# Written program order for the load queue and GpSimd, projection weights asked for one by one, and no emptying of the list of score portions at a period's end

## The chip, the cores and the metric

One Trainium2 chip; the kernel runs on one core of it. The metric is the device time of one execution in microseconds (us), as the median over several executions. In what follows PE is TensorE, DVE is VectorE, ACT is ScalarE, POOL is GpSimd, and SP is SyncE, which here only issues DMAs: it is the queue of nearly all loads.

## What is computed

Two cross-attention layers over 8 batches (B) of 100 queries (S) with 640 channels (C), 20 heads of 32, all in float32. The context has 722 tokens of 1024 channels, of which the first 77 are text and the other 645 image tokens ("ip"), with their own key and value weights. Layer 0 is

```python
q = heads(x @ Wq.T)
out_text = attend(q, heads(text @ Wk.T), heads(text @ Wv.T), 1 / sqrt(D))
out_ip   = attend(q, heads(ip @ Wk_ip.T), heads(ip @ Wv_ip.T), 1 / sqrt(D))
out = (out_text + out_ip) @ Wo.T + bo + x
```

with `attend` a softmax over the keys and the product with the values. Layer 1 does the same with its own weights on layer 0's output, with two differences: to the scores of the image tokens it adds a term that is the same for all heads (a softmax of the text attention over all channels, carried over to the image tokens by their products with the text), and a mask of the 100 queries multiplies the image part.

## The kernel before

**Units and periods.** A unit is a layer with a batch: 16 of them (`u`), each with five chunks of four heads (`c`), so 80 periods (`ORDER`, L44). The main loop (L1571 to L1661) goes through the periods. In each, it does the attention of one chunk, and between its pieces it places a share of the products that make the later units' keys and values.

**Products.** Keys and values of the image tokens are made by a scheme of seven products in place of eight, used twice: an outer one (`OUTER`) over quarters of the operands, and within it `seven` (L152). `v_steps` (L465, matmuls at L479) and `k_steps` (L516, matmuls at L525) are its inner products, `fifth_steps` (L541, L554) do what is left over. Sums of input tokens are DVE's (L258 to L264, L281 to L287), the results leave PSUM through ACT (L176) and DVE (L179), and the outer sums are POOL's (L441). POOL's queue also writes the finished keys and values to DRAM (`put`, from L381) and the sums of weights (`ol_d`, `tx_d` and the like) in the first stage.

**Loads.** Weights stream through six buffers of the tag "w"; `take` (L314) asks for weights up to five ahead of the one that PE is about to use, all on SP (L329, L348, L361, L375). In layer 0 some of them get a second DMA into the same tile, the text columns (L340). SP also loads token tiles (`load_a`, L235 and L238), q of a unit (`load_q`, L1106), text values (L1112, L1113), keys and values of a period (`load_k`, L1120 and L1121, with two buffers; `load_v`, L1126), and projection weights (`load_wo`, L1212), which `out_piece` (L1215) and `q_piece` (L1235) use through three buffers of the tag "wo". Where SP reaches a DMA whose buffer or source isn't ready, it waits, and every load behind it waits too.

**Who sets the order.** The program is written under `manual_schedule(engines=PINNED)` (L1039 for the first stage, L1571 for the body). For the engines in `PINNED` (L47) the instructions run in the order in which the program asks for them; for the others a scheduler chooses. Before, PE, DVE and ACT are pinned, and SP and POOL are not.

**A period.** `scores` (L1300) part 0 makes the scores of the first 512 keys of four heads, part 1 those of the other 210 (133 image and 77 text). Each part uses the same two tiles of PSUM banks, `sc0` and `sc1`, for two heads each, so the next part's matmuls (L1312) wait until all that reads the former part's banks is done. Right behind the matmuls only `maxima(0)` is asked for (layer 0: a reduction, L1321; layer 1: a fused add, minimum and accumulate into `p`, L1327). The rest is put into the list `later` as portions with a flag. The flag is true where the portion reads the `sc` banks:

- part 0: `maxima(1)` (true), exponentials of heads 0 and 1 (true), of heads 2 and 3 (true; ACT, L1335)
- part 1: `maxima(1)` (true), text maxima with differences and exponentials (true; L1342, L1344, L1351, L1352), exponentials of heads 2 and 3 with those of the text (true in layer 0 alone; L1335, L1357, L1360), the last text exponentials (true in layer 0 alone), `factors` (false; L1367 to L1371), and `widened` with `scaled_rest` (false; POOL L1377, ACT L1388, DVE L1383)

`next_task` (L1579) asks for one portion whenever products of 1.0 us or more, by the planner's own costs, have gone by since the last one. `free_scores` (L1296) asks for all up to the last one that is flagged true. The transposes of the former period's probabilities go to PSUM in six steps (`transposes`, L1432; copied out by ACT at L1440 for steps 0, 2, 4 and 5, by DVE at L1442 for steps 1 and 3), and `values` (L1444, matmuls L1454) multiplies them with the values; its results go through DVE (L1459, L1460). A period is, in this order: scores part 0; products up to 0.4; transposes 0 and 1 of the former period; products up to 0.6; transposes 2 and 3; scores part 1; products up to 0.8; the loads of this period's values and the next one's keys; transposes 4 and 5; products up to 1.0; values of the former period. In the last periods there are no products.

Before, the list is emptied three times in a period: ahead of transposes 0 (`emit(len(later))` at L1424), ahead of the values (L1650) and behind them (L1653); `free_scores` is called ahead of the second scores only.

## Time and profile before

| | |
|---|---|
| median of 3 runs | 2092.13 us (2086.02 to 2099.58) |
| profiled execution | 2102.3 us; span 2100.5 us; mean granted clock of TensorE 0.979 |
| PE busy | 1971.8 us (94%) |
| first stage of sums and text products, and units ahead of the body | 0 to about 552 us |
| body, layer 0 | about 552 to 1449 us (40 periods) |
| body, layer 1 | 1449 us to the end (40 periods) |
| DMA | 419.13 MB, mean 200 GB/s |

The page first gives each engine's busy time, then the span in 40 slices of 52.5 us, in which a digit is the busy share in tenths; PEclk is the clock that TensorE was granted, in tenths of full speed. A line of a group reads: line, engine, operation, output and inputs, shape, count, then busy time, mean ns of one, and idle time of the engine just ahead of them with what ended it. A line of waits reads: who waited, for what, then total us, times, and the longest. The two busy PE figures by stage, from a table of windows: 277.80 us of the 331 from 219 to 550 us (clock 0.94), 871.06 of the 899 from 550 to 1449 us (clock 0.99), 607.05 of the 651 from there to 2100 us (clock 0.98).

### The profile page before, as it was taken

How to read it: one execution, taken by the hardware profiler on the slowest of the kernel's cores; microseconds unless marked ns; L12 is line 12 of the kernel's file. 1: busy time of each engine (PE TensorE's matmuls, PEld its weight loads, DVE VectorE, ACT ScalarE, POOL GpSimd, SP SyncE). 2: the span in 40 equal slices, each digit the busy share in tenths (PEclk: the TensorE clock that was granted, in tenths of full speed). 3: DMA queues.
4: the chain of work that ended last, by engine and by line, in shares of the span. 5: the costliest groups of instructions: out<-in, count | busy, mean ns of one | idle time of the engine just before them, and what ended most of it. 6: DMA issues, size and time to landing. Idle time of an engine off the chain costs nothing. (4 is left out here: it accounts for less than half of the span.)

```text
span 2100.5 us, 43283 instructions
## 1 busy us (share of the span) xinstructions
PE 1971.8 (94%) x15422; PEld 1608.4 (77%) x15422; DVE 1231.7 (59%) x3047; ACT 829.0 (39%) x2839; POOL 1039.9 (50%) x1256
## 2 busy tenths in 40 slices
PE   9999876899999999999999999999999999999998
PEld 8676765787777788778788888887877777676787
DVE  2322673554655754665457666657676666766666
ACT  1001000010244443544354435445554555556665
POOL 2788887545456452644445674663455355210110
PEclk9999998999999999999999999999999999999999
DMA  9577887777666667766776676666766666554441
GB/s 350 204 264 262 263 278 231 199 215 213 201 183 197 201 178 205 212 189 181 204 226 197 205 216 205 202 204 177 211 187 200 178 200 194 149 159 119 137 132 53
DMA packets 439600, 419.13 MB, mean 200 GB/s; under 512 B 67691, under 2 KB 381819, under 8 KB 439131
## 3 DMA queue, kind: packets, MB, share of 16 engines
q1 hardware_dynamic: 407982, 306.67, 50.7%
q0 software_dynamic: 26400, 101.03, 13.4%
q10 hardware_dynamic: 5004, 8.68, 1.1%
q8 instruction: 124, 2.03, 0.4%
q14 instruction: 90, 0.73, 0.1%
HBM read 315.07 MB, written 101.18 MB: 198 GB/s over the span
## 5 line engine op out<-in xcount | busy, mean ns | idle before, releaser
L441 POOL TENSOR_TENSOR cv<-cv,cv 128x320 f32<-128x320 f32 x252 | 219.7, 897 | 305.0 <-DVE cv L179 280.3
L1440 ACT COPY pt<-pspt 128x400 f32<-128x400 f32 x320 | 156.1, 491 | 226.2 <-PE pspt L1432 225.5
L441 POOL TENSOR_TENSOR ck<-ck,ck 128x256 f32<-128x256 f32 (+1 forms) x252 | 201.0, 803 | 67.9 <-DVE ck L179 44.4
L1432 PE MATMUL pspt<-ident,p 100*128 100x100 f32 (+1 forms) x1920 | 210.1, 252 | 19.3 <-ACT pt L1440 7.1
L1432 PEld LDWEIGHTS pspt<-ident,p 100*128 100x128 f32 (+1 forms) x1920 | 189.4, 139 | 50.5 <-issue 14.9
L1335 ACT ACTIVATE p<-sc,st 100x512 f32<-100x512 f32 (+1 forms) x320 | 166.6, 533 | 71.5 <-DVE st L1342 49.2
L1335 ACT ACTIVATE p<-p,st 100x512 f32<-100x512 f32 (+1 forms) x320 | 177.1, 557 | 11.7 <-DVE st L1327 9.3
L1377 POOL COPY wide<-st 100x128 f32<-100x128 f32 x80 | 30.4, 380 | 292.8 <-DVE st L1371 265.2
L479 PE MATMUL psv_d<-w,i 128*128 128x160 f32 (+1 forms) x1008 | 170.0, 312 | 3.2 <-DMA w<-text_t 1.0
L479 PEld LDWEIGHTS psv_d<-w,i 128*128 128x128 f32 x1008 | 154.3, 193 | 14.8 <-issue 3.0
L176 ACT COPY cv<-psv_a 128x320 f32<-128x320 f32 x126 | 53.7, 426 | 262.6 <-PE psv_a L479 241.7
L1312 PE MATMUL sc<-k,q 32*100 32x210 f32 (+1 forms) x1280 | 149.2, 507 | 8.2 <-ACT p L1360 7.0
L176 ACT COPY ck<-psk_a 128x256 f32<-128x256 f32 (+1 forms) x126 | 47.2, 374 | 256.9 <-PE psk_a L525 209.1
L1388 ACT ACTIVATE p<-p,st 100x133 f32<-100x133 f32 x316 | 102.3, 395 | 115.5 <-DVE st L1371 115.4
L525 PE MATMUL psk_d<-i,w 128*128 128x256 f32 (+1 forms) x504 | 134.6, 390 | 10.6 <-DMA w<-op_dk 6.0
L1327 DVE CUSTOM_DVE_ANT_0 p<-sc,sem 100x512 f32<-100x512 f32 (+1 forms) x320 | 139.5, 489 | 1.3 <-PE sc L1312 1.3
L1442 DVE COPY pt<-pspt 128x400 f32<-128x400 f32 x160 | 91.6, 573 | 73.6 <-PE pspt L1432 72.7
L1321 DVE TENSOR_REDUCE st<-sc 100x2 f32<-100x1024 f32 (+1 forms) x160 | 126.6, 824 | 7.7 <-PE sc L1312 7.3
L525 PEld LDWEIGHTS psk_d<-i,w 128*128 128x128 f32 x504 | 92.5, 192 | 37.4 <-issue 16.2
L479 PE MATMUL psv_a<-w,a 128*128 128x160 f32 (+1 forms) x576 | 107.1, 330 | 5.2 <-DVE ck L179 5.0
L179 DVE TENSOR_TENSOR cv<-psv_d,cv 128x320 f32<-128x320 f32 x126 | 61.6, 489 | 82.0 <-PE psv_d L479 80.7
L479 PEld LDWEIGHTS psv_a<-w,a 128*128 128x128 f32 x576 | 93.7, 196 | 12.3 <-DVE ck L179 5.3
(278 smaller groups left out, 4409.6 us busy)
## 6 DMA issues: line engine op xcount, KB each, us to landing
w<-op_dv SPq DMA_DIRECT2D x252, 160.0 KB
a<-ip_t SPq DMA_DIRECT2D x33, 1024.0 KB
w<-op_dk SPq DMA_DIRECT2D x252, 128.0 KB
k<-k_d SPq DMA_DIRECT2D x80, 322.5 KB
v<-v_d SPq DMA_DIRECT2D x80, 320.0 KB
v_d<-cv POOLq DMA_DIRECT2D x28, 640.0 KB, 4.9
w<-os_dv SPq DMA_DIRECT2D x108, 160.0 KB
k_d<-ck POOLq DMA_DIRECT2D x28, 512.0 KB, 4.5
```

The lines of the kernel that those rows point to most:

```text
L176: nc.scalar.copy(c11, flat(bank))
L441: nc.gpsimd.tensor_tensor(to[:, a, b], of[:, a, b], other[:, a, b], ALU.add)
L479: nc.tensor.matmul(ps[:, o * pitch : o * pitch + m], lhsT=of[:, kc, o * w : o * w + P], rhs=wt[:, kc, :], start=(o == 0 and kc == 0 and no ...
L525: nc.tensor.matmul(ps[:, : 2 * w], lhsT=wt[:, kc, :], rhs=of[:, kc, :], start=(kc == 0 and not go_on), stop=(kc == 1), skip_group_check=True,)
L1312: nc.tensor.matmul(scs[i // 2][:S, i % 2, : k1 - k0], lhsT=qs_[u][rows, c, :], rhs=ks[u, c][rows, k0:k1], start=True, stop=True)
L1321: nc.vector.tensor_reduce(st[:, part, 2 * h : 2 * h + 2], scs[h][:S, :, :n], AX.X, ALU.max, negate=True)
L1327: nc.vector.tensor_tensor_reduce(out=p[:, i, k0 : k0 + n], in0=scs[h][:S, i % 2, :n], in1=sems[u][:, k0 : k0 + n], scale=-1.0, scalar=3.0e ...
L1335: nc.scalar.activation(dst, dst if l else scs[h][:S, i % 2, :n], AF.Exp, bias=st[:, part, i : i + 1], scale=-1.0 if l else 1.0, accum_out= ...
L1388: nc.scalar.activation(p[:, i, KA:NI], p[:, i, KA:NI], AF.Copy, scale=mul[:, 1, i : i + 1])
L1432: nc.tensor.transpose(ps[:rows, i * S : (i + 1) * S], pr[u, c][:, i, j * P : j * P + rows], ident[:S, :S])
L1440: nc.scalar.copy(dst, src)
L1442: nc.vector.tensor_copy(dst, src)
```

## The change

Three parts.

1. `PINNED` holds SP and POOL as well: their DMAs and POOL's sums run in the written order.
2. `load_wo` puts its weights on a list `wo_next`, and `fill_wo` issues a load only while one of three places is free; a place becomes free when `out_piece` or `q_piece` has been asked for. Before, all of a group's loads were asked for at once, and the scheduler placed them. The loads of one group come at the start of periods 0 and 1 of an even unit (`loads`, L1543).
3. `scores` calls `free_scores` ahead of both parts. The list is no longer emptied ahead of transposes 0, nor around the values, except in the last period.

```diff
-PINNED = {mybir.EngineType.PE, mybir.EngineType.DVE, mybir.EngineType.Activation}
+PINNED = {
+    mybir.EngineType.PE, mybir.EngineType.DVE, mybir.EngineType.Activation, mybir.EngineType.SP, mybir.EngineType.Pool
+}
...
+    wo_next, wo_free = [], [3]
+
     def load_wo(kind, src, g, chunks=range(NC_)):
-        for c in chunks:
+        wo_next.extend((kind, src, g, c) for c in chunks)
+        fill_wo()
+
+    def fill_wo(done=0):
+        wo_free[0] += done
+        while wo_next and wo_free[0]:
+            kind, src, g, c = wo_next.pop(0)
+            wo_free[0] -= 1
             t = one.tile([P, NC_, P], F32, tag="wo", name=f"{kind}_{g}_{c}", bufs=3)
...
             nc.gpsimd.dma_start(x1_d[g], res)
+        fill_wo(1)
...
             nc.gpsimd.dma_start(q_d[1][g], qst[g])
+        fill_wo(1)
...
             stats[u, c] = stat.tile([S, 11, 4], F32, tag="st", name=f"st_{u}_{c}")
-        else:
-            free_scores()
-
+        free_scores()
...
     def transposes(u, c, j, at_end=False):
         if j == 0:
-            emit(len(later))
             pts[u, c] = one.tile([P, 6, 4 * S], F32, tag="pt", name=f"pt_{u}_{c}")
...
-            emit(len(later) - (n == len(ORDER) - 1))
+            if n == len(ORDER) - 1:
+                emit(len(later) - 1)
             if last:
                 values(*last)
-            emit(len(later))
+            if n == len(ORDER) - 1:
+                emit(len(later))
             last = (u, c)
```

## The prediction

> **What bounds the kernel now.** I read the page's busy shares first, then its slices, then the groups of instructions, the waits of TensorE (PE), the timeline of one period and the waits of the load queue (SP).

> ```profile
> span 2100.5 us, 43283 instructions
> PE 1971.8 (94%) x15422; PEld 1608.4 (77%) x15422; DVE 1231.7 (59%) x3047; ACT 829.0 (39%) x2839; POOL 1039.9 (50%) x1256
> PE   9999876899999999999999999999999999999998
> PEclk9999998999999999999999999999999999999999
> ```
> PE is the bound: 94% busy at full clock nearly everywhere, no other engine over 59%. Only slices 5 to 8 (about 210 to 420 us) show room. So a wait that the change puts on PE is paid in full, and little can be won.

> ```profile
> PE psv_e L479 <- DMA w<-op_dv: 22.5, 6, 15.2
> PE sc L1312 <- ACT p L1360: 7.0, 5, 2.1
> PE sc L1312 <- DVE st L1327: 1.2, 2, 0.6
> ```
> Adding up PE's gaps: 124 us in 101, of which 53 us in 219–550 us (45 us on loads) and some 68 us behind it, 41 us on DVE and 15 us on ACT. The scores (L1312) wait for nearly nothing in 160 instances: their banks are free in time.

> ```profile
> L1327 DVE CUSTOM_DVE_ANT_0 p<-sc,sem 100x512 f32<-100x512 f32 x160 | 101.4, 684 | 0.6 <-PE sc L1312 0.6
> L1442 DVE COPY pt<-pspt 128x400 f32<-128x400 f32 x160 | 91.6, 573 | 73.6 <-PE pspt L1432 72.7
> ```
> These are what can come between PE and its next scores: the maxima of layer 1 and the copy of a transposed tile.

> ```profile
> 1508.51 0.91 PE L1432 MATMUL pspt<-ident,p 100*128 100x100 f32 x8
> 1509.35 0.61 PE L1312 MATMUL sc<-k,q 32*100 32x210 f32 x8
> 1509.45 0.57 DVE L1442 COPY pt<-pspt 128x400 f32<-128x400 f32 x1 [0.72 <-PE pspt L1432]
> 1509.99 0.30 DVE L1327 CUSTOM_DVE_ANT_0 p<-sc,sem 100x133 f32<-100x133 f32 x1
> ```
> Today the second scores follow the transposes without a gap: all four maxima of the first part were done long before.

> **The change, part by part.** PE's order is the same instruction by instruction; on DVE, ACT, POOL and SP the counts stay and the order moves.

> *Portions: scores, part 1, layer 1.* The emptying at L1424 came ahead of transposes 0. Without it a portion is asked for only per 1.0 us of product, and layer 1's periods are shorter (40 in 651 us, against 40 in 897 us). Following the list through the loop, task by task with the planner's own times (0.87 to 1.35 us a product, so at most one portion for two), the second maxima of part 0 are still unasked at `scores(…, 1)` in 33 of 40 periods. `free_scores` asks for them there, so on DVE they stand behind the copy of transposes 3, which ends 0.60 us after those transposes. Two maxima at 0.61 us pace and the last read make 1.30; the first two heads' scores (0.28) run meanwhile: 0.60 + 1.30 − 0.28 = 1.6 us for PE. Where leftovers of the period before are ahead of them, DVE does those first: L1383 adds 0.47, the whole of L1367 to L1383 1.6 us (1800.80 to 1802.40). By lists: 9 × 1.65, 3 × 2.1, 18 × 3.2, 3 × 4.2, and 1.7 in the rest = **+93 us**. Below: 33 × 1.0 if DVE runs ahead (33); above: 40 × 4.2 (168). I take 93, from this row's own pace.

> *Scores, part 0, layer 1.* In 11 periods text maxima are left over, and stand on DVE behind the two hs operations (L1459, L1460), which wait for the values: 7 × 1.7 + 4 × 1.2 = 17, less 2 of cover: **+15** (0 to 30).

> *Layer 0.* At part 1, exponentials are left in 11 periods. ACT does four at 0.73 us behind the copy of transposes 2: 6 × 1.3 + 3 × 2.7 + 2 × 3.1 = 22, and 2 at part 0: **+24** (0 to 40; the waits on L1360 today, 1.4 us each, are the low side).

> *Last eight periods.* No products lie between, so transposes 4 and 5 wait for what ACT is asked for late (four L1388 at 0.32 pace, exponentials): **+10** (0 to 20).

> *Clock.* Of about 25 gaps of 1.6 us or more in this trace, 16 are followed by a stretch at half clock, for instance after the 2.48 us that ended at 1426.58:
> ```profile
> 1426.00:1428.00 2.00, 1.42 (x8) 1.11 (x8) 2.00 (x6) 1.77 (x5) 1.40 (x1) 0.92 0.01 4
> 1428.00:1430.00 2.00, 1.95 (x8) 1.89 (x8) 2.00 (x3) 0.48 (x2) 2.00 (x3) 0.50 0.33 80
> 1430.00:1432.00 2.00, 2.00 (x13) 1.99 (x12) 1.36 (x4) 0.24 (x1) 1.39 (x2) 0.73 0.06 18
> ```
> The last but two column is the clock. Such a stretch of some 3.4 us loses 1.7. The parts above make about 38 such gaps; 38 × 16/25 × 1.7 = **+41 us** (0 to 65).

> [...]

> *What goes.* The burst at a period's end put maxima, exponentials, factors and scaling on DVE and ACT at once, ahead of values. The gaps behind 550 us that DVE and ACT end are 56 us, with some ten clock drops. I take half of the gaps and a few drops: **−35** (0 to −60).

> *SP and GpSimd in written order; what stands behind each wait.*
> ```profile
> SPq L340 <- DMA w<-op_dv: 32.9, 29, 3.2
> SPq L1106 <- DMA ol_d<-olv: 15.5, 1, 15.5
> SPq L1120 <- PE sc L1312: 95.3, 67, 8.5
> SPq L1126 <- PE pv L1454: 78.7, 65, 15.0
> SPq L1212 <- PE pspt L1432: 39.9, 24, 4.8
> ```
> Each of these holds every later load. (a) q's load (L1106) blocks SP for 15.5 us and gave PE its longest gap, 15.16 at 342.08. In the written order it stands further back, but still ahead of a unit's weights, and its source is still written by POOL behind four adds of 0.87 and eight of 0.69: some 12 us of block in place of 15. (b) The block of 299–317 us (4.25 + 3.24 + 3.64 = 11 us) comes from two activations' loads held by DVE; they now stand together: about 4 us. (c) The text columns (L340) stand right behind their weight's load, into the same tile; each holds SP for 2.7 us (750.63 to 753.31). Four in a row outrun a look-ahead of five weights when products are 2.4 us: +10 in the first stage, 0 to 5 in the body, where I take 0. (a) to (c) with other first-stage loads that move: **−8** (−28 to +15). (d) k (L1120) is asked for at 0.8 of the period before, and comes 4.3 to 6 us before its scores, where v and k (643 KB) need 4 us if they flow at the 161 GB/s that layer 1 moves in the mean, and 5.5 if a quarter of that is weights (an estimate): **+3** (0 to 25). (e) A projection weight (L1212) now waits for its piece at most some 3 us, which five weights of look-ahead cover: **0** (0 to 3); cover gone, its cost is those 3 us per piece.

> **Sum.** 93 + 15 + 24 + 10 + 41 − 35 − 8 + 3 = +143 us. The profiled execution took 2102.3 (span 2100.5, 1.8 around it), 0.5% above the runs' median of 2092.1. 2102.3 + 143 = 2245; against the median **2235**.

> **The rivals.**
> *1. Faster: the end of the period gives more than the scores take.* If the new stalls in layer 1 are 1 us with their clock in place of (93 + 41)/33 = 4.1, because DVE reaches the copy before PE has need of it, they cost 33; 15 of the smaller stalls stay; the burst's gaps and drops go whole (56 + 10 × 1.7 = 73), and 8 on SP: 33 + 15 − 73 − 8 = −33, **2060**. It decides below about 2 us per stall. For it: DVE is only 59% busy, and 41 us of gaps end on DVE. Against: the copy cannot start before PE has done transposes 3, and PE's next instruction are the scores.
> *2. The clock holds.* As the main case without the 41: **2194**. For it: a third of today's gaps cost no clock; against: the row above.
> *3. SP becomes the bound.* k late by 25 us in all, text columns +5, the first stage at +15: 143 − 3 + 25 + 5 + 23 = +193, **2285**. For it: one queue, with 67 waits of L1120; against: SP's waits today end before PE's need nearly always.
> *4. Nothing much.* If portions were still asked for in time the rest is −8 + 3 and the time stays at **2090**. The order on DVE speaks against it.

> **How the numbers follow.** Main case 0.53, rival 2 0.20, rival 3 0.10, rival 1 0.10, rival 4 0.07. The likeliest gives 2235. The range leaves out rivals 1 and 4 and the outer part of 3: from 2115 (the low ends of the scores and the clock: 33 + 0 + 10 + 0 + 0 − 20 = +23) to 2290. About 1% is what a measurement of this kernel can tell from no change: faster 0.10, same 0.07, slower 0.83.

> **What would show it.** Right: PE's sc L1312 waiting on DVE L1327 some 35 times for about 90 us; some 20 us of sc on ACT L1335; a clock below 0.95 in slices from about 1450 us; one long L1106 wait in the first stage; waits of PE on DVE and ACT in products (ck, cv L179) down. Wrong: sc's waits under 1 us each; no half clock behind them; or PE's gaps in layer 1 ended by DMA (k, w), which would be rival 3.

## The result and the profile after

| | before | changed |
|---|---|---|
| median of 4 runs each | 2095.86 us (2086.02 to 2100.02) | 2377.03 us (2372.31 to 2381.6) |
| ratio | | 1.1349, 95% interval 1.1296 to 1.1402 |
| profiled execution: span, mean granted clock | 2100.5 us, 0.979 | 2371.4 us, 0.932 |

The changed kernel is 13.5% slower, 281 us by the medians. The forecast was 2235 us, with a range up to 2290: the direction was right, the rise that it gave was half of the measured one, and 2377 us lies above the range. Lines of the changed kernel have other numbers: L479 is L481, L340 is L342, L1106 is L1108, L1312 is L1323, L1327 is L1338, L1432 is L1442, L1442 is L1452.

The page of the changed kernel, top and slices:

```profile
span 2371.4 us, 43269 instructions
PE 2092.5 (88%) x15422; PEld 1692.2 (71%) x15422; DVE 1231.6 (52%) x3047; ACT 825.7 (35%) x2839; POOL 1025.7 (43%) x1256
PE   9999989786889998998899989999898998888877
PEclk9999999988999998999999999999999999888877
```

PE does the same 15422 instructions in 2092.5 us of busy time where it took 1971.8. DVE, ACT and POOL are as busy as before to within 1.5%. So PE has lost time in two ways: it waits more, and the same work takes longer. The clock row says why the work takes longer: in the last six slices it stands at 8 or 7, where it was 9 before.

The waits of PE in the changed kernel (who waited, for what; us in total, times, longest):

```profile
PE sc L1323 <- DVE st L1338: 87.8, 34, 3.8
PE sc L1323 <- DMA k<-k_d: 28.6, 14, 5.7
PE psv_e L481 <- DMA w<-tx_d: 22.0, 7, 7.5
PE psv_a L481 <- DMA w<-text_t: 21.4, 2, 20.3
PE sc L1323 <- ACT p L1346: 19.7, 17, 1.8
PE sc L1323 <- issue: 12.2, 7, 1.8
```

The scores, which waited for nearly nothing before, now have four main causes of waiting. To see the whole, I added up PE's idle time stage by stage, and the clock that was not granted ("clock lost": one minus the clock, added up over time, so that a microsecond at half clock counts 0.5):

| stage | before | changed | longer by | more idle | more clock lost |
|---|---|---|---|---|---|
| ahead of the first scores | 551 us | 575 us | 23 | 15 | 12 |
| layer 0 | 894 | 986 | 92 | 60 | 31 |
| layer 1, 32 periods | 547 | 640 | 93 | 44 | 43 |
| last 8 periods | 108 | 170 | 62 | 32 | 32 |
| sum | 2100.5 | 2371.4 | 271 | 150 (129 to 279) | 117 (45 to 162) |

The two columns account for 267 of the 271 us (stage by stage to within 6). One second score of layer 1 shows both losses. First the timeline, from the transposes to the scores (start, duration, engine, line; brackets: idle ahead of it):

```profile
1611.22 0.85 PE L1442 MATMUL pspt<-ident,p 100*128 100x100 f32 x8
1612.01 0.60 PE L1323 MATMUL sc<-k,q 32*100 32x210 f32 x4
1612.11 0.57 DVE L1452 COPY pt<-pspt 128x400 f32<-128x400 f32 x1 [1.96 <-PE pspt L1442]
1612.61 0.47 DVE L1378 TENSOR_REDUCE st<-p 100x4 f32<-100x308 f32 x1
...
1613.76 0.47 DVE L1394 TENSOR_TENSOR p<-p,st 100x308 f32<-100x308 f32 x1
1614.15 0.68 DVE L1338 CUSTOM_DVE_ANT_0 p<-sc,sem 100x512 f32<-100x512 f32 x1
...
1615.50 1.02 PE L1323 MATMUL sc<-k,q 32*100 32x210 f32 x4 [2.90 <-DVE st L1338]
```

The first two heads' scores go ahead. DVE, which had idled for 1.96 us, then does the copy, the factors, and only then the two maxima that free the other bank: 2.90 us for PE. Next the same place in stretches of 3.41 us (length, PE's busy time first, the granted clock third from the end):

```profile
1610.86:1614.27 3.41, 1.75 (x16) 1.25 (x14) 2.05 (x8) 1.17 (x4) 0.30 (x1) 1.00 0.98 339
1614.27:1617.68 3.41, 2.18 (x8) 1.64 (x9) 2.13 (x12) 3.41 (x11) 0.11 (x1) 0.50 0.11 41
1617.68:1621.10 3.42, 3.42 (x11) 3.06 (x11) 0.40 (x1) 0.79 (x3) 0.35 (x1) 0.50 0.27 72
1621.10:1624.51 3.41, 3.41 (x28) 3.38 (x28) 0.03 (x1) 1.84 (x7) 3.41 (x5) 1.00 0.71 229
```

The one gap lies in two of these stretches, 1.66 us in the first and 1.23 in the second, and each is followed by one at half clock. The gap cost 2.90 us of idle and 3.4 of clock.

### The profile page after: what moved, and what is told of

Same layout as the page of the kernel before. It is cut to its first block, busy times and chain, and to the rows that moved or that the text cites. A ratio compares the mean times of both kernels' runs of the same rounds, so it can differ in the third digit from the quotient of the medians.

```text
span 2371.4 us, 43269 instructions
## 1 busy us (share of the span) xinstructions
PE 2092.5 (88%) x15422; PEld 1692.2 (71%) x15422; DVE 1231.6 (52%) x3047; ACT 825.7 (35%) x2839; POOL 1025.7 (43%) x1256
## 5 line engine op out<-in xcount | busy, mean ns | idle before, releaser
L1323 PE MATMUL sc<-k,q 32*100 32x210 f32 (+1 forms) x1280 | 191.7, 541 | 163.3 <-DVE st L1338 87.8
L1442 PEld LDWEIGHTS pspt<-ident,p 100*128 100x128 f32 (+1 forms) x1920 | 197.8, 143 | 33.6 <-issue 20.2
L1442 PE MATMUL pspt<-ident,p 100*128 100x100 f32 (+1 forms) x1920 | 216.6, 258 | 1.4 <-DVE ck L181 0.4
L1323 PEld LDWEIGHTS sc<-k,q 32*100 32x100 f32 x1280 | 64.3, 169 | 208.5 <-DVE st L1338 99.8
L443 POOL TENSOR_TENSOR ck<-ck,ck 128x256 f32<-128x256 f32 (+1 forms) x252 | 187.1, 773 | 21.4 <-DVE ck L181 20.9
L481 PE MATMUL psv_d<-w,i 128*128 128x160 f32 (+1 forms) x1008 | 179.6, 324 | 13.4 <-DMA w<-op_dv 5.6
L1388 POOL COPY wide<-st 100x128 f32<-100x128 f32 x80 | 29.9, 374 | 367.3 <-DVE st L1382 327.6
L481 PEld LDWEIGHTS psv_d<-w,i 128*128 128x128 f32 x1008 | 162.8, 202 | 28.7 <-issue 13.8
L1332 DVE TENSOR_REDUCE st<-sc 100x2 f32<-100x1024 f32 (+1 forms) x160 | 129.7, 824 | 75.0 <-PE sc L1323 73.6
L1338 DVE CUSTOM_DVE_ANT_0 p<-sc,sem 100x512 f32<-100x512 f32 (+1 forms) x320 | 141.5, 489 | 33.6 <-PE sc L1323 33.0
L1452 DVE COPY pt<-pspt 128x400 f32<-128x400 f32 x160 | 91.5, 573 | 95.8 <-PE pspt L1442 94.9
L481 PE MATMUL psv_a<-w,a 128*128 128x160 f32 (+1 forms) x576 | 110.8, 338 | 22.9 <-DMA w<-text_t 20.3
L481 PEld LDWEIGHTS psv_a<-w,a 128*128 128x128 f32 x576 | 97.3, 202 | 30.2 <-issue 21.7
```

What stands on the lines that cost most here:

```text
L443: nc.gpsimd.tensor_tensor(to[:, a, b], of[:, a, b], other[:, a, b], ALU.add)
L481: nc.tensor.matmul(ps[:, o * pitch : o * pitch + m], lhsT=of[:, kc, o * w : o * w + P], rhs=wt[:, kc, :], start=(o == 0 and kc == 0 and no ...
L1323: nc.tensor.matmul(scs[i // 2][:S, i % 2, : k1 - k0], lhsT=qs_[u][rows, c, :], rhs=ks[u, c][rows, k0:k1], start=True, stop=True)
L1332: nc.vector.tensor_reduce(st[:, part, 2 * h : 2 * h + 2], scs[h][:S, :, :n], AX.X, ALU.max, negate=True)
L1338: nc.vector.tensor_tensor_reduce(out=p[:, i, k0 : k0 + n], in0=scs[h][:S, i % 2, :n], in1=sems[u][:, k0 : k0 + n], scale=-1.0, scalar=3.0e ...
L1442: nc.tensor.transpose(ps[:rows, i * S : (i + 1) * S], pr[u, c][:, i, j * P : j * P + rows], ident[:S, :S])
```

## The experiments

Times are medians; "before" was run on the same chip each time, and ratios and differences to "before" are to that.

### Which part costs what

**queues_only**: the changed kernel with the three old emptyings put back, and `free_scores` ahead of the second scores only.

> The changed kernel with the old emptying of the list (ahead of transposes 0, around the values; free_scores ahead of the second scores only): only the queues' order and the projection weights' places differ from before. Theory now (two separate costs): the written order of SP costs what the changed kernel shows outside of the second scores: the body begins 23 us later (574.6 in place of 551.2), k is late by 28 us in layer 0, and the clock behind those gaps loses some 20: 23 + 28 + 20 = +71, about 2165 us; the scores wait for DVE under 5 us. Rival (the queue is late only because the portions stall PE and POOL): within 1% of before, 2075 to 2115 us, and k waits under 5 us.

Measured: 2193.2 us, ratio 1.0424 (1.0385 to 1.0463).

```profile
PE sc L1325 <- DMA k<-k_d: 32.3, 19, 6.0
PE psv_e L481 <- DMA w<-tx_d: 23.5, 8, 7.0
PE psv_a L481 <- DMA w<-text_t: 20.9, 3, 19.3
```

What has grown here is waiting for loads: PE's waits for DMA add up to 108 us, against 56 before, and the second scores' waits for the maxima stay at 1.2 us. The body begins at 571 us, and 29 us more clock is lost than before. The queues' order costs by itself, as the theory had it, and more than it said (92 us against 71). This run holds the projection weights' new places too, and no run has them alone. They are unlikely to carry it: SP's waits at them are 71 us here against 75 before, and PE waits for none of them in the changed kernel.

**portions_only**: the kernel before with the third part alone.

> The kernel before with the third part of the change alone (no emptying, free_scores ahead of both scores); SP and POOL stay with the scheduler. Theory: the second scores wait for DVE about 90 us in 34 times, for ACT about 20 us in 17, and the clock behind these gaps loses some 80 us more than before; the stalls of products on DVE fall by 30: 2096 + 90 + 20 + 20 + 80 - 30 = about 2275 us. Rival (the gaps cost no clock by themselves, the clock fell because SP's gaps come on top): 2096 + 100 = about 2195 us, clock at or over 0.96.

Measured: 2304.2 us, ratio 1.0952 (1.0919 to 1.0985), clock 0.939.

```profile
PE sc L1310 <- DVE st L1325: 89.1, 34, 3.8
PE sc L1310 <- ACT p L1333: 20.2, 18, 1.8
```

The waits come out as in the changed kernel, without its queues. 97 us more clock is lost than before, where 80 was expected. By the medians, 92 + 203 = 295 us for the two sides, queues and portions, against 281 for both: they are nearly independent, and the portions are two thirds of the loss.

### The portions

**emptied0**: the changed kernel with `emit(len(later))` back ahead of transposes 0.

> The changed kernel with one line put back: the list is emptied ahead of transposes 0. Theory: the second maxima then stand on DVE ahead of the copy again, the second scores' waits on DVE (88 us) and ACT (20 us) go to under 10 us, and with them some 75 us of clock: 2377 - 100 - 75 = about 2200 us. Rival (the stall only moves: transposes 0 and 1 or their copies then wait as long for DVE and ACT, as the list holds the leftovers there too): a gain of under 40 us, 2340 us or more.

Measured: 2287.0 us, between the two. The second scores' waits on DVE fall to 5 us, and on ACT to 1, but only half of the expected gain comes, as other waits have grown:

```profile
PE pspt L1443 <- DVE pt L1453: 17.5, 16, 2.7
```

Emptied at that place, the leftovers stand ahead of the next copies, and the transposes wait for those instead. With the list emptied at the period's end as well, as in queues_only, these waits are 5.0 us in 4, as before the change.

**max_now**: the changed kernel, with the second maxima of the first scores asked for at once in layer 1.

```diff
         maxima(0)
-        later.append((True, lambda: maxima(1)))
+        if l and part == 0:
+            maxima(1)
+        else:
+            later.append((True, lambda: maxima(1)))
```

> The changed kernel with the second maxima of the first scores in layer 1 asked for at once behind the first ones, and no longer through the list. Theory (it is these two instructions' place behind the copy that makes the second scores wait): PE's waits of sc for DVE fall from 88 us to under 15, and with them half of the 90 us of clock that layer 1 loses: 2377 - 75 - 50 = about 2250 us. Rival (what is left on the list, factors and exponentials, stalls the second scores or the products just as long): waits of PE on DVE in layer 1 of 60 us or more, wherever they stand, and over 2330 us.

Measured: 2302.6 us, again between the two. The 32 periods of layer 1 take 569 us in place of 640 (before: 547), and lose 15 us of clock in place of 53: there the place of these two instructions was the cause. The last eight periods gain only 7 us, since another wait takes the place. Both in PE's waits:

```profile
PE sc L1323 <- DVE st L1338: 0.6, 1, 0.6
PE pspt L1445 <- ACT p L1399: 15.4, 8, 2.6
```

The second are the scalings on ACT ahead of transposes 4 and 5, which the longer wait for DVE had covered.

**split_end**: the kernel before, with the burst at a period's end thinned out.

```diff
-                if later and since[0] >= 1.0:
+                if later and since[0] >= 0.5:
...
-            emit(len(later) - (n == len(ORDER) - 1))
+            if n == len(ORDER) - 1:
+                emit(len(later) - 1)
+            else:
+                free_scores()
             if last:
                 values(*last)
-            emit(len(later))
+            if n == len(ORDER) - 1:
+                emit(len(later))
```

> The kernel before with the portions eased in another way: at a period's end only those that free the scores' banks are asked for, the factors and the scaling stay on the list, one portion goes with every product, and the list is still emptied ahead of transposes 0. Theory (the burst at the end costs the 30 us of PE's waits for DVE and ACT in layer 1 with 10 of clock): these waits fall by half and the time to 2070 to 2090 us. Rival (what stays on the list is in the way of the copies at transposes 0, as in the run with the list emptied there): waits of transposes for copies of 20 us or more in layer 1 and no gain, 2100 to 2140 us.

Measured: 2138.9 us, ratio 1.0202 (1.0170 to 1.0235): the rival. Transposes wait 29 us for copies. But by stages, layer 0 took 883 us in place of 894, and layer 1 and its last periods took 571 and 130 in place of 547 and 108. That led to the next two.

**split_first**: the same in layer 0 only (layer 1 keeps both emptyings at the end), one portion per product in both layers.

> The kernel before with the eased portions in layer 0 only (at a period's end what frees the banks, the rest with the products), one portion for every product in both layers; layer 1 keeps the burst at the end. In the run with the eased portions everywhere, layer 0 took 883 us in place of 894 and layer 1 571 in place of 547. Theory (layer 0 has products enough to spread the list, layer 1 has not): layer 0 keeps the 11 us and layer 1 stays at 547: 2085 us, 0.5% faster. Rival (the 11 us came by chance from the first stage's state, or go back in layer 1): within 4 us of before.

Measured: 2083.7 us, ratio 0.9924 (0.9904 to 0.9944), 0.8% faster than the kernel before. Layer 0 took 881 us and layer 1's 32 periods 540.

**split_first_slow**: as split_first with the old pace of one portion per 1.0 us.

> As the run with the eased portions in layer 0 only, but with a portion per 1.0 us of product as before. Theory (pace matters, as lists of up to four portions are left at transposes 0 otherwise): layer 0 gains less, 4 to 8 us, 2090 us. Rival (pace does not matter): the same time as with one for every product, within 3 us.

Measured: 2113.9 us, ratio 1.0073 (1.0053 to 1.0093); layer 0 took 906 us. Neither expectation holds: without the faster pace the same split is slower than the kernel before. My reading is that a list that is not emptied needs a pace at which it runs empty by itself. The faster pace with all the old emptyings was not run, so how much of split_first's gain is due to the pace alone is not shown.

### The clock

**filled**: the changed kernel with extra transposes behind transposes 3 of layer 1, where three portions are left.

> The changed kernel with extra transposes on PE behind transposes 3 in layer 1, where the list holds three portions ahead of the second scores: 4, 6, 10 or 14 of about 0.23 us each, by how much DVE has to do first, into columns of the PSUM tile that nobody reads. They wait for DVE's copy (0.6 us) and then work while PE would wait, so they take no time by themselves, and they are work that the result does not need. Theory (an idle PE costs clock afterwards): idle at the second scores falls from 88 to about 35 us, the half-clock stretches behind them go, and the time falls by 40 to 70 us to 2305 to 2340 us although PE does more. Rival (the clock falls for another reason than the gaps): the time stays at 2377 us or rises by up to 20, with as many stretches at half clock.

Measured: 2370.5 us: as the rival had it. But the filling waited for the copy, for 26 us in all, and the second scores still waited 30 us for DVE, so too much idle was left to tell.

**filled_dense**: matmuls of 128x128 by 128 in the second scores' first bank, which wait for nothing.

```diff
+    FILLS = (6, 8, 12, 12, 16)
...
+        flags = [r for r, _ in later]
+        fills = FILLS[flags.index(True)] if part and u >= B and sum(flags) >= 3 else 0
         free_scores()
         scs = [ps_sc.tile(...) for h in range(2)]
+        for _ in range(fills):
+            nc.tensor.matmul(scs[0][:, 0, :P], lhsT=ident, rhs=ident, start=True, stop=True)
```

> The changed kernel with extra matmuls of 128x128 by 128 columns ahead of the second scores in layer 1, into the first scores' bank, which they overwrite: 6, 8, 12 or 16 of them where the list still holds three portions. They wait for nothing, fill the wait at the scores from its start, and are work that the result does not need. In the runs so far the clock changes only on a grid of 3.41 us, and after a window with under 1 us of idle it stays full. Theory (what counts is the work of PE in a window): idle at the second scores of layer 1 falls from 88 to under 25 us, and of the 90 us of clock that layer 1 loses at least half comes back: 2377 - 45 = 2330 us or less. Rival (windows with transposes and scores are too thin anyway, and filling does nothing, as with the extra transposes): 2360 us or more.

Measured: 2342.2 us, ratio 1.1157 (1.1112 to 1.1202) against 1.1349. The wait at the second scores fell from 88 to 10 us,

```profile
PE sc L1329 <- DVE st L1344: 10.2, 22, 2.7
```

and the clock lost in layer 1 (last eight periods included) from 90 to 33. PE does 83 us more of work, and the kernel is 35 us faster. The clock did what the theory had said; the time stayed 12 us above its 2330.

**filled_thin** and **filled_thin2**: the same place with transposes of 100x128, first as many as the matmuls, then about as much time.

> As the changed kernel filled with matmuls of 128x128 by 128 ahead of the second scores, but with as many transposes of 100x128 by 100 at the same place, into the same bank, waiting for nothing: the same gaps are filled, with thinner work. It is work that the result does not need. Theory A (idle time in a window of 3.41 us is what counts): the clock loss of layer 1 falls as with the dense filling, from 90 to about 35 us, and the time to about 2340 us. Theory B (the work done counts, and transposes count for little): the clock loss of layer 1 stays over 65 us and the time over 2360 us.

Measured: 2366.7 us. These transposes filled only 35 us, 58 us of waiting for DVE stayed, and 78 us of clock was lost. That can be read either way.

> As the run with thin transposes ahead of the second scores of layer 1, but 14, 19, 28 or 38 of them in place of 6, 8, 12 or 16: in that run one took 0.10 us where one of the 128x128 matmuls took 0.24 us, so it filled 35 us of the waits where those filled 83 and left 60 us of idle. Now the filled time is the same as with the matmuls. It is work that the result does not need. Theory A (idle time in a window of 3.41 us is what counts): idle at the second scores falls to about 12 us, the clock loss of layer 1 from 90 to about 35 us, and the time to about 2340 us. Theory B (the kind of work counts, and transposes count for little): idle falls as far, but the clock loss of layer 1 stays over 65 us and the time over 2360 us.

Measured: 2341.7 us, waits of 18 us, 30 us of clock lost: theory A. Last the slices' clock in filled_thin and in filled_thin2:

```profile
PEclk9999989998999998999999999999999998899877
```

```profile
PEclk9999999988999998999899999999999999999988
```

Layer 1 begins at slice 27. More of the same transposes, with less idle left, lost 30 us of clock in layer 1 where the matmuls lost 33: in this run they did not count for little. That the kind of work makes no difference is not shown: behind stretches with 1 to 2 us of idle the outcome goes with it, 191 of 305 against 76 of 600 (see the last section).

### The queues

**text_late**: the changed kernel with the text columns issued two weights later.

```diff
+    behind, LATE = [], 2
...
             streamed[0] += 1
+            while behind and behind[0][0] <= streamed[0] - 1 - LATE:
+                behind.pop(0)[1]()
+        while behind and behind[0][0] <= at:
+            behind.pop(0)[1]()
...
-                nc.sync.dma_start(t[:, :, HV:], src)
+                behind.append((streamed[0], lambda: nc.sync.dma_start(t[:, :, HV:], src)))
```

> The changed kernel with the text columns' load issued two weights later on SP instead of right behind their weight, so that SP need not wait for that weight to land. Theory (SP's waits at the text columns, 184 us in 64, are what makes k and weights late): these waits fall under 60 us, PE's waits for k from 29 to under 8, for tx_d and text columns (without the one of 20 us behind q) from 25 to under 10: 35 us idle and 25 us of clock, 2377 - 60 = about 2315 us. Rival (k and weights are late since too many bytes are asked for at once): waits for k at 20 us or more, time 2360 or more.

Measured: 2335.7 us, ratio 1.1133 (1.1092 to 1.1174). SP's waits at the text columns fell from 184 to 38 us, and

```profile
PE sc L1328 <- DMA k<-k_d: 11.5, 12, 2.1
```

In the changed kernel, the waits for keys (28.6 us) were mostly the text columns' doing. Two thirds of the expected gain came.

**k_early**: the changed kernel with the next keys asked for right behind the first scores.

> The changed kernel with the next period's keys asked for right behind a period's first scores instead of at 0.8 of it. Theory (k is late because it is asked for late in the written order): waits for k fall from 29 us to under 3, and with their clock the time falls by 35 to 45 us to about 2337 us. Rival (whatever stands behind on SP comes late instead: k only changes place with weights or values): k waits go, but waits of products for weights rise by 20 us or more, and the time stays over 2365 us.

Measured: 2356.8 us. The waits for k are gone, but PE's other waits for loads in layer 0 rose from 15 to 29 us. Both are half right: the keys had been asked for late, and something else is late instead.

**q_later**: the changed kernel with q's first load 0.3 of a period's products ahead of the body.

> The changed kernel with the first loads of q, text values and k asked for 0.3 of a period of products ahead of the body instead of ahead of all of the body's products. Theory (q's load stands on SP for 17 us behind POOL's last write of ol_d, and all weights behind it): PE's gap of 20.3 us goes, with some 6 us of clock: about 2350 us, body beginning at about 550 us. Rival (the wait only moves: the next load to use that memory, or q itself, comes late at the first scores): over 2368 us, with a gap of 8 us or more at the first scores.

Measured: 2373.9 us. The gap of 20 us is gone and the body begins at 563 in place of 575 us, but waits for k rose to 34.6 us and the time stays. Inconclusive by itself.

**sp_only**: queues_only with POOL left to the scheduler.

> The kernel with the queues' part alone, but POOL left to the scheduler and only SP in written order. Theory (the load queue carries the queues' cost, as the text columns and the late keys are SP's): as with both, 2193 us within 15, k waits about 28 us. Rival (POOL's written order, which delays the writes that loads wait for, carries it): 2150 us or less.

Measured: 2171.0 us, ratio 1.0352 (1.0311 to 1.0393). Against its own before that is 76 us, so SP, with the projection weights' places, carries most of the 92. The other 16 would be POOL's order, near the 15 that the theory allowed; the two intervals overlap, so this share is uncertain.

**queues_fixed**: queues_only with text_late and q_later.

> The kernel with the queues' part alone, the text columns issued two weights later, and q's first load 0.3 of a period's products ahead of the body. Theory (these are the two places where SP stands for nothing): 40 us back for the text columns, as with the changed kernel, and 10 for q: 2193 - 50 = about 2143 us; SP's waits at the text columns under 60 us. Rival (the scheduler's order has other merits, such as keys asked for early, and that is what is lost): 2175 us or more.

Measured: 2127.1 us, ratio 1.0145 (1.0108 to 1.0182). That is 32 us over its own before, so the two places together are worth 60 of the queues' 92 us. That is some 17 more than the text columns gave in the changed kernel. That these are q's is likely, for PE's gap of 19.3 us ahead of the body is gone, but it is not shown by a run of its own on this base. The body begins at 546 us, earlier than before (551), and what is left is mostly layer 0's waits for keys and weights:

```profile
PE sc L1330 <- DMA k<-k_d: 24.6, 17, 5.9
```

On this base the keys stay late: 24.6 us of waits in place of 32.3, though SP's waits at the text columns fell from 188 to 33 us. So the text columns explain the late keys of the changed kernel, but not most of them here. What holds the keys here is not shown.

## Why the prediction was right, and where it was wrong

The terms in the prediction's order, with what the changed kernel's trace gives for each:

| term | forecast | measured | |
|---|---|---|---|
| second scores of layer 1 behind the copy | +93 | +87 (34 waits, last eight periods included) | right; max_now shows the cause |
| first scores of layer 1 | +15 | +18, of which 12 with no releaser shown | size right in part by luck: the cause named shows for 6 |
| layer 0, exponentials | +24 | +21 | right |
| last eight periods, transposes 4 and 5 | +10 | 0 | hidden behind the scores' waits; 15 us of it came out in max_now |
| what goes: waits of products and transposes on DVE and ACT | -35 | -30 | right |
| SP: first stage, with layer 0's weights | -8 | +24 | wrong |
| keys late | +3 | +29 | wrong, just over its upper end of 25 |
| clock | +41 | +117 | wrong, 76 us short |

Together that is 266 of the 271 us.

**The step that failed most is the clock.** The prediction put it so: "The parts above make about 38 such gaps; 38 × 16/25 × 1.7 = +41 us (0 to 65)". That gaps cost clock is right: filled_dense and filled_thin2 do nothing but close gaps, and the clock lost in layer 1 fell from 90 to 33 and 30 us. The size failed, and most of all the price of an episode at half clock. portions_only has the gaps that the term counted, without those of the queues: 29 episodes more than before, where 38 × 16/25 = 24 were forecast, and 97 us of clock lost, so 3.3 us an episode in place of 1.7. The trace before could have warned: its 18 episodes last 5.1 us in the mean and not 3.4. The traces show three reasons. First, the edges of the clock lie on a grid of 3.41 us, and the clock of a stretch went with the idle in the stretch ahead (see the last section). So the gap of 2.90 us above, which lies across an edge with 1.66 us on one side and 1.23 on the other, was followed by two stretches at half clock, and gaps under 1.6 us count too: 9 of the changed kernel's 58 episodes begin behind a stretch with no longer gap. Second, a stretch at half clock with 0.25 to 1.0 us of idle was followed by another one in 145 of 170 cases: four times in the last eight periods half clock held for three or four stretches in a row, 10.2 to 13.7 us. Third, the gaps of the queues (first stage and keys) were costed at none, and queues_only alone loses 29 us of clock.

**The second is SP.** Step (c) said that a text column's load holds SP for 2.7 us and then took "0 to 5 in the body, where I take 0". The price was right for the written order: in the changed kernel these 64 waits take 184 us, 2.9 in the mean, in place of 66. (In the trace before, SP issued two other weights in the 2.7 us that the prediction quotes, so there SP was not held for all of them.) What failed is that the look-ahead would cover them, for the keys of layer 0 stand behind them. The longest waits come behind a token load of 1 MB: the eight with one among the six loads ahead take 5.8 us in the mean, up to 9.4, the other 56 take 2.5. One of the eight:

```profile
609.36 0.45 SPq L331 DMA_DIRECT2D w<-op_dv  x1
614.62 0.37 SPq L342 DMA_DIRECT2D w<-tx_d  x1
615.04 1.38 SPq L331 DMA_DIRECT2D w<-wvi  x1
616.47 0.46 SPq L1128 DMA_DIRECT2D v<-v_d  x1
617.03 0.47 SPq L1122 DMA_DIRECT2D k<-k_d  x1
```

From one weight's issue to its text columns 5.26 us go by. PE is done with the work ahead of the scores at 615.13, their keys are asked for at 617.03, and the scores begin at 620.78. In text_late SP's waits at the text columns fall to 38 us. Step (a) put q's block at 12 us; SP's one wait there (L1108, for `ol_d`) took 17.2, and PE's gap behind it 20.3. Step (b) came out in part: of its three gaps, 11 us together, one of 2.5 is left, but another of 6.1 stands at 314.9. Step (e) had the cost right, none that shows, but not the waits: SP's waits for the projection weights' buffers reach 19.5 us in place of 3, and no gap of PE for a load follows the three longest. Step (d) had a slip, too: 643 KB at three quarters of 161 GB/s need 5.3 us and not 5.5; it changes nothing.

**The rivals.** "The clock holds" is refuted by the half-clock stretches: 58 episodes against 18 before. "SP becomes the bound" was right in direction: its 25 us for late keys came (28.6), and its time of 2285 was the nearest of all. But it kept 41 for the clock, and its sign, waits for DMA in layer 1, did not show: the keys are late in layer 0. "Faster" failed where the prediction said: the copy can't begin before the transposes are done (in the timeline above DVE idled 1.96 us until then). "Nothing much" fell with the waits at the second scores.

## What to carry to other kernels

In a list of deferred work, what frees the next matmul's buffer must be asked for ahead of anything that waits for the matmuls just before it; count what is left on the list at that place, period by period, before dropping an emptying, and raise the pace at the same time. When the bounding engine is TensorE, cost a stall at its idle time plus the clock behind it, here 117 us on 150. In a queue that is run in written order, a load that must wait for its neighbour's landing holds every load behind it (here 184 us in 64 waits, and 38 us with the text columns two weights later), so let some others go between.

## What the runs showed of the hardware

| stretch ahead | idle in it | followed by half clock |
|---|---|---|
| full clock | under 1.0 us | 0 of 8282 |
| full clock | 1.0 to 2.0 us | 267 of 905 |
| full clock | 2.0 us or more | 396 of 396 |
| half clock | under 0.25 us | 77 of 715 |
| half clock | 0.25 to 1.0 us | 145 of 170 |
| half clock | 1.0 us or more | 198 of 198 |

So full clock was kept behind under 1.0 us of idle in all 8282 cases and lost behind 2.0 us or more in all 396; half clock ended behind under 0.25 us in 638 of 715 and behind 1.0 us or more in none of 198. At full clock and between 1.0 and 2.0 us the kind of work in the stretch goes with the outcome. With less than 1 us of scores and transposes in it, 76 of 600 were followed by half clock; with 1 us or more, 191 of 305. At nearly the same idle, 1.25 to 1.5 us, it was 0 of 181 and 54 of 86. Why, these runs can't tell.
